# A two-layer graph attention kernel: one of seven products made with seven smaller ones, a bias put into the accumulators, ELU plus one, masks in halves and another schedule

## The chip, the cores and the metric

The kernel runs on one core of one Trainium2 chip. A core has TensorE (matmuls; PE in the profile, with its weight loads as PEld), VectorE (DVE), ScalarE (ACT), GpSimd (POOL) and SyncE (SP). Matmuls write to PSUM, eight banks of 512 f32 columns on 128 partitions; everything else lies in SBUF. The metric is device time in microseconds of one whole execution, for 32 graphs.

## The reference

```python
h = relu(layernorm(x))                 # x: (32, 512, 512) f32, adj: (32, 512, 512) int32
mask = (adj > 0) | eye(512)
def gat_layer(x, mask, W, a_src, a_dst, bias, concat):
    xl = (x @ W).reshape(B, N, H, F)
    e = leaky_relu(asrc[:, :, None, :] + adst[:, None, :, :], 0.2)   # asrc = <xl, a_src>, adst = <xl, a_dst>
    attn = softmax(where(mask, e, -1e9), axis=1)
    out = einsum('bsdh,bshf->bdhf', attn, xl)
    return out + bias                   # heads side by side if concat, else their mean
h = elu(gat_layer(h, mask, W1, ..., b1, concat=True))    # 4 heads of 256: 512 -> 1024
out = x + gat_layer(h, mask, W2, ..., b2, concat=False)  # 1 head: 1024 -> 512
```

All arithmetic on the large matrices is f32.

## The kernel before, in words

One graph is a batch of 512 nodes, held as four tiles of 128 rows. Per batch there are four large matrix products: the first projection (512 x 512 by 512 x 1024), the gather of layer 1 (per head, attention 512 x 512 by features 512 x 256), the second projection (512 x 1024 by 1024 x 512) and the gather of layer 2 (512 x 512 by 512 x 512). Two scalars per head, the scores of the attention, come out of the projections as extra columns, so the first has 258 columns per head and the second 257 per half.

**Seven products.** Each of these is cut into 2 x 2 blocks and made with seven block products instead of eight (Strassen's scheme in Winograd's form). `sums` makes the four sums of the left blocks (s1 = a21 + a22, s2 = s1 - a11, s4 = a12 - s2, and a21 becomes a11 - a21); `sums_of_weights` makes those of the weights once. `sevens` (line 814 on) runs over pairs of a unit (which part of the block's rows and columns) and a product number: a product is `kh` matmuls of 128 x 128 weights by 256 to 258 columns, two deep in the first projection and in the gathers, four deep in the second projection. Products share three accumulators per unit: 1, 6, 7, 4 go into bank `a`, 5 and 3 into `b`, 2 into `g`. After every product its partial sum is evicted to SBUF: products 1, 4, 5 and 6 by a ScalarE copy into their block (with sign -1 in the projections), 2, 3 and 7 by a VectorE addition or subtraction onto theirs. Batch 0 alone has its first projection and gather in plain form (`project1_first`, `gather1_plain`).

**The order.** The program first writes down all jobs with their reads, writes and an estimated cost (`prog.add`, by the helpers `act` at line 379, `dve` at 382, `dma` at 385, `accumulate` at 390 and `pe` at 396, which is why nearly all instructions of the profile carry one of these lines). TensorE keeps the written order. For the other engines and the two DMA queues (SyncE's, and GpSimd's for accumulating DMAs) `Program.order` simulates the chip with the costs, tries orders forwards and backwards, and keeps the one in which TensorE's products come soonest. The result is a fixed instruction stream per engine. It models DMAs as one wire with a lead and a tail:

```python
DMA_LEAD, DMA_TAIL, AHEAD = 0.8, 2.0, 3.5
```

PSUM banks come from a queue of eight: the one that was given back longest ago is taken first.

**Stages around the change.** In the main loop, round i does the second layer of batch i, the first gather of batch i+1 in pairs of heads (`PAIRS_OF`), the first projection of batch i+2 and the normalisation of batch i+3. Of the projection's 28 products, 14 run before the second pair of heads is gathered and 14 after it, in the order `FOUR`: two units, then two more.

- `masks` (line 504) turns four adjacency tiles into 0 or -2^100 in bf16 (`m`), sets the diagonal, writes the whole mask to DRAM (`dm`), and transposes it in two DMAs into `mt`. The transposed one enters the column minimum in `Soft.first`; the one in DRAM is added to the scores by GpSimd's accumulating DMAs in `Soft.second`. For the last batch VectorE adds `m` itself.
- `Soft.spread` writes small score vectors to DRAM (`das`, `drr`) and reads them back as rows on all partitions (`as`, `rr`), through SyncE's queue.
- `elu` (line 923): `h1` holds a gathered head with its sign changed; ScalarE makes exp(b1 - h1), then relu(1 - that), and VectorE min(h1 - b1, that), which is -elu. The following projection changes the sign back.
- `residual` (line 1104) loads the rows of x and VectorE adds b2 to them (`t<-t,b_sb`), 0.6 us each; `gather2` adds the gathered sums to them and stores them.

Of the kernel before, what the change touches and what calls it, by code (L numbers as in the profile page):

```python
# [10 lines left out]
F32 = mybir.dt.float32  # L11
# [8 lines left out]
P = 128  # L20
# [23 lines left out]

class Program:
# [9 lines left out]
    DMA_LEAD, DMA_TAIL, AHEAD = 0.8, 2.0, 3.5  # L55
# [28 lines left out]
    def forwards(self, rank):  # L84
# [5 lines left out]
        ready_at, start, landed = [0.0] * n, [0.0] * n, 0.0  # L90
        free, soon, ready = defaultdict(float), defaultdict(list), defaultdict(list)
        tensor = deque(j for j in range(n) if jobs[j][0] == "PE")
        for j in range(n):
            if not left[j] and jobs[j][0] != "PE":
                heappush(soon[jobs[j][0]], (0.0, j))
        done = []
        while len(done) < n:
            j, t = self.next_job(rank, free, soon, ready, tensor, left, ready_at, landed - self.AHEAD)
            start[j] = t
            free[jobs[j][0]] = t + jobs[j][1]  # L100
            done.append(j)
            if jobs[j][4] is not None:
                landed = max(landed, t + jobs[j][1] + self.DMA_LEAD) + jobs[j][4]
            for s in after[j]:
                if jobs[j][4] is not None:
                    r = landed + self.DMA_TAIL
                else:
                    r = t + jobs[j][1] + self.latency(j, s)
# [3 lines left out]
                if not left[s] and jobs[s][0] != "PE":  # L112
                    heappush(soon[jobs[s][0]], (ready_at[s], s))
        return start, done, cause
# [18 lines left out]
    def backwards(self, rank):  # L133
# [9 lines left out]
        while True:  # L143
            for j in found:
                if jobs[j][4] is not None:
                    moving = max(moving, ready_at[j]) + jobs[j][4]
                    ready_at[j] = moving + self.DMA_LEAD
# [4 lines left out]
            j, t = self.next_job(rank, free, soon, ready, tensor, left, ready_at)  # L152
# [4 lines left out]
            for d in jobs[j][2]:  # L157
                later = self.DMA_TAIL if jobs[d][4] is not None else self.latency(d, j)
# [5 lines left out]
    def next_job(self, rank, free, soon, ready, tensor, left, ready_at, hold=0.0):  # L164

        best = None
        for e in ("PE", "ACT", "DVE", "POOL", "SP"):
# [10 lines left out]
            if e in ("SP", "POOL"):  # L178
                t = max(t, hold)
            if best is None or t < best[0]:  # L180
                best = (t, e)
        t, e = best
        if e == "PE":
            return tensor.popleft(), t
# [3 lines left out]
        return heappop(ready[e])[1], t  # L188
# [3 lines left out]
    def order(self):  # L192
# [8 lines left out]
        for j in reversed(range(n)):  # L201
            later = self.DMA_LEAD + self.DMA_TAIL + (jobs[j][4] or 0.0)
# [54 lines left out]
def tile_gat(  # L257
# [75 lines left out]
    b1_sb = sbuf.tile([P, 2, FT], F32, name="b1_sb")  # L333
    b2_sb = sbuf.tile([P, DO], F32, name="b2_sb")
# [5 lines left out]
    hs = sbuf.tile([P, 3, KH, N // 2], F32, name="hs")  # L340
# [3 lines left out]
    xrs = slots("xr", 4, [P, N])  # L344
# [1008 lines left out]
```

## Time and profile before

| | |
|---|---|
| median of 3 runs | 2785.93 us (2783.84 to 2788.35) |
| profiled execution, first to last instruction (span) | 2778.8 us |
| median less span | 7.1 us |
| TensorE busy, records | 2746.2 us, 12520 |
| VectorE busy, instructions | 2645.4 us, 6726 |
| ScalarE busy, instructions | 2304.3 us, 4870 |
| GpSimd busy | 324.7 us |
| granted TensorE clock, mean | 0.998 |
| DMA moved | 501.55 MB |

The page gives one execution's span and no other time of it; what lies around the span (7.1 us to the median) is start and end of the program. An f32 matmul shows as two records. A record lasts about 380 ns, but the next starts some 217 ns later, so the busy time of an engine is the union of its records, and the distance between starts is what an instruction really costs. VectorE and ScalarE instructions overlap in the same way, by about 0.1 us. A group's row gives the names of what is written and read (numbers left out), the shape, busy time, the mean of one, and the idle time just before, with what ended it; `w_sb` stands for either weight, `h` for `h1`.

### The profile page before, as it was taken

The page shows a single profiled execution, that of the slowest core. Times are in us where ns is not written, and L with a number is a line of the kernel's source. Part 1 is how long each engine was busy: PE and PEld are TensorE (multiplying, and loading weights), DVE is VectorE, ACT ScalarE, POOL GpSimd, SP SyncE. Part 2 cuts the span into 40 slices and gives each one's busy share as a digit, 9 for nine tenths or more (in the row PEclk, how much of TensorE's full clock was granted, in tenths as well). Part 3 has the DMA queues.
Part 4 walks back from the last instruction along what each step waited for, and adds up shares of the span by engine and source line. Part 5 has one row for each costly group of instructions (what it writes and reads, how often), then busy time and mean ns, then how long its engine had stood idle before and what let it go on. Part 6 is the DMA issues. An engine that isn't in the chain of part 4 may idle for free. (4 is left out here: it accounts for less than half of the span.)

```text
span 2778.8 us, 41571 instructions
## 1 busy us (share of the span) xinstructions
PE 2746.2 (99%) x12520; PEld 2373.9 (85%) x12520; DVE 2645.4 (95%) x6726; ACT 2304.3 (83%) x4870; POOL 324.7 (12%) x356
## 2 busy tenths in 40 slices
PE   7999999999999999999999999999999999999999
PEld 6688888888888888888888888888888888888887
DVE  7999999999999999999999999999999999998997
ACT  5988888889888888888888888888888888887883
POOL 0110111001111101111011101011110111101110
PEclk9999999999999999999999999999999999999999
DMA  7766767667777667676677766777666867678663
GB/s 228 171 176 178 201 174 199 171 175 181 191 194 174 179 165 203 177 186 184 172 192 184 196 168 175 178 189 195 183 175 175 202 166 202 157 189 182 169 158 107
DMA packets 370964, 501.55 MB, mean 180 GB/s; under 512 B 222260, under 2 KB 226868, under 8 KB 370740
## 3 DMA queue, kind: packets, MB, share of 16 engines
q1 hardware_dynamic: 324948, 332.16, 43.6%
q0 software_dynamic: 45792, 166.74, 25.2%
q8 instruction: 100, 1.64, 0.2%
q14 instruction: 124, 1.02, 0.1%
HBM read 315.89 MB, written 51.31 MB: 132 GB/s over the span
## 5 line engine op out<-in xcount | busy, mean ns | idle before, releaser
L396 PE MATMUL mm<-w_sb,hs 128*128 128x257 f32 (+2 forms) x3032 | 688.5, 381 | 4.9 <-DVE hs L382 2.5
L396 PEld LDWEIGHTS mm<-w_sb,hs 128*128 128x128 f32 x3032 | 575.8, 190 | 92.0 <-ACT xl L379 4.6
L390 POOL DMA_DIRECT2D p<-dm x314 | 276.2, 887 | 2346.3 <-DVE p L382 1600.3
L379 ACT ACTIVATE l<-as,z 128x512 f32<-128x512 f32 x640 | 442.8, 721 | 101.9 <-DMA as<-das 96.2
L379 ACT ACTIVATE l<-l,low 128x512 f32<-128x512 f32 x640 | 459.2, 721 | 49.1 <-DVE low L382 46.0
L396 PE MATMUL mm<-w_sb,ht 128*128 128x258 f32 x2112 | 481.4, 382 | 1.9 <-DVE xl L382 1.4
L396 PE MATMUL mm<-p,xl 128*128 128x256 f32 (+1 forms) x1984 | 468.0, 384 | 1.0 <-DVE h L382 0.8
L396 PE MATMUL mm<-w_sb,h 128*128 128x257 f32 x2056 | 467.8, 379 | 0.0
L379 ACT ACTIVATE p<-p,z 128x512 f32<-128x512 f32 (+1 forms) x636 | 427.2, 716 | 42.6 <-DMA p<-dm 28.1
L382 DVE SCALAR_TENSOR_TENSOR p<-rr,z 128x512 f32<-128x512 f32 (+1 forms) x636 | 449.0, 743 | 11.8 <-DMA rr<-drr 11.6
L396 PEld LDWEIGHTS mm<-w_sb,ht 128*128 128x128 f32 x2112 | 400.9, 190 | 61.8 <-DVE xl L382 4.1
L382 DVE CUSTOM_DVE_ANT_1 l<-l,mt 128x512 f32<-128x512 f32 x640 | 429.1, 685 | 12.0 <-ACT l L379 9.5
L396 PEld LDWEIGHTS mm<-w_sb,h 128*128 128x128 f32 x2056 | 389.4, 189 | 57.8 <-issue 0.5
L396 PEld LDWEIGHTS mm<-p,xl 128*128 128x128 f32 x1984 | 377.1, 190 | 61.7 <-issue 5.7
L379 ACT ACTIVATE xl<-mm 128x258 f32<-128x258 f32 (+2 forms) x748 | 279.8, 382 | 70.6 <-PE mm L396 68.7
L379 ACT ACTIVATE h<-mm 128x256 f32<-128x256 f32 x496 | 181.7, 378 | 91.0 <-PE mm L396 88.4
L382 DVE TENSOR_TENSOR xl<-xl,mm 128x258 f32<-128x258 f32 x558 | 222.8, 420 | 29.1 <-PE mm L396 24.3
L379 ACT ACTIVATE xr<-h,b_sb 128x512 f32<-128x512 f32 x248 | 176.7, 721 | 75.7 <-DVE h L382 72.0
L396 PE MATMUL mm<-t,hs 128*128 128x256 f32 x992 | 226.0, 380 | 2.9 <-ACT h L379 2.9
L396 PEld LDWEIGHTS mm<-t,hs 128*128 128x128 f32 x992 | 188.4, 190 | 29.9 <-ACT h L379 4.7
L382 DVE SCALAR_TENSOR_TENSOR h<-h,b_sb,xr 128x512 f32<-128x512 f32 x248 | 182.9, 747 | 3.2 <-ACT xr L379 3.1
L382 DVE TENSOR_TENSOR t<-mm,t 128x256 f32<-128x256 f32 (+1 forms) x424 | 172.8, 419 | 11.7 <-PE mm L396 10.5
(114 smaller groups left out, 3421.8 us busy)
## 6 DMA issues: line engine op xcount, KB each, us to landing
p<-dm POOLq DMA_DIRECT2D x314, 512.0 KB, 5.2
rr<-drr SPq DMA_DIRECT2D x159, 512.0 KB
x<-in_x_dram SPq DMA_DIRECT2D x129, 256.0 KB
adj<-in_adj_dram SPq DMA_DIRECT2D x128, 256.0 KB
as<-das SPq DMA_DIRECT2D x64, 512.0 KB
t<-in_x_dram SPq DMA_DIRECT2D x124, 256.0 KB
out_dram<-t SPq DMA_DIRECT2D x124, 256.0 KB
dm<-m SPq DMA_DIRECT2D x32, 512.0 KB
```

What stands on the lines that cost most here:

```text
L379: prog.add("ACT", cost, reads, writes, lambda: nc.scalar.activation(*a, **k))
L382: prog.add("DVE", cost, reads, writes, lambda: f(*a, **k))
L390: lambda: nc.gpsimd.dma_start(to, at, accum_op=OP.add), size,
L396: f(*a, **k)
```

## The change

- **First projection.** Product 2 (a12 by b21, 256 x 256 by 256 x 516) is not made as four units of two matmuls any more, but itself with seven smaller products (`low`), one matmul of 128 x 128 by 258 columns each. `low_weights` makes the sums of b21's blocks once, `low_sums` those of a12's blocks per batch on VectorE, 128 columns each. Three parts (two units and `low`) now run interleaved in the order `TOP`; 19 of 31 products come before the second pair of heads. For the second pair of units the results of product 2 wait in `later`, and product 1 of those units is added to them by VectorE. Where a further bank is free, the sum of the small product 1 is copied to it by ScalarE (`forked`).
- **Second bias in banks.** b2 is no longer added to x on VectorE. ScalarE copies it (`seeds`) into the banks of products 1 and 5 of the second projection, and these products add to it. Since the features are gathered with weights that sum to one, a bias on the features is a bias on the result. `bias2` corrects it once by the column sums of W2, with 16 matmuls.
- **ELU plus one.** The eviction of layer 1 applies the sign and b1 + 1; `elu` is then one Exp on ScalarE and one VectorE step, max(h1, min(exp(h1 - 1), 1)) = elu + 1. The Relu pass is gone. The added one is what the column sums of W2 correct.
- **Masks in halves.** `m` holds two tiles instead of four; each half is written to DRAM and transposed by itself, and an accumulating DMA waits only for its half. The last batch reads its mask back from DRAM (`m_last`).
- **s4 after s2.** In the second projection and the gathers s4 overwrites s2, after product 6 has read it.
- **Schedule.** The planner models two DMA wires that share bandwidth, with other leads, tails, transfer costs and a hold on how far ahead DMAs are issued. `Banks` takes a bank by the width that was last written. There are three `xr` buffers instead of four, and `gather2` takes its products in the order `NEAR`.

```diff
+class Banks:
...
+    def __init__(self, tiles):
+        self.tiles, self.free, self.wide = tiles, deque(range(len(tiles))), [0] * len(tiles)
+    def take(self, width=512, kept=0):
+        i = next((i for i in self.free if self.wide[i] >= kept), None)
+        if i is None:
+            return None
+        self.free.remove(i)
+        self.wide[i] = max(width, self.wide[i] if kept else 0)
+        return ("mm", i), self.tiles[i]
+    def give(self, key):
+        self.free.append(key[1])
...
     PAIRS = {("PE", "ACT"): 0.21, ("PE", "DVE"): 0.21, ("DVE", "POOL"): 0.58, ("POOL", "DVE"): 0.4}
-    DMA_LEAD, DMA_TAIL, AHEAD = 0.8, 2.0, 3.5
+    DMA_LEAD, DMA_TAIL, AHEAD = {"SP": 0.6, "POOL": 0.75}, {"SP": 1.2, "POOL": 1.2}, 3.5
+    ALONE = {"SP": 1.0, "POOL": 1.0}
+    SHARED = {0: {"SP": 0.44, "POOL": 0.62}, 1: {"SP": 0.3, "POOL": 0.62}}
+    TURN = 0.95
...
+    def low_weights():
+        r00, r10, r11 = (w1_sb[:, 1, k, j, :] for k, j in ((0, 0), (1, 0), (1, 1)))
+        t1, t2, t4 = (w1_low[:, i] for i in range(3))
+        sub = nc.vector.tensor_sub
+        dve(ADD, R_KEYS, ["low1"], sub, t1, R01, r00)
+        dve(ADD, [*R_KEYS, "low1"], ["low2"], sub, t2, r11, t1)
+        dve(ADD, R_KEYS, R_KEYS, sub, R01, r11, R01)
+        dve(ADD, [*R_KEYS, "low2"], ["low4"], sub, t4, r10, t2)
...
+    def low_sums():
+        (a11, a12), (a21, a22) = (
+            [(ht[:, KQ + k, m * P : (m + 1) * P], [("ht", m, 1)]) for k in range(KQ)] for m in range(2)
+        )
+        s1, s2, s4 = ((hl[:, i], [("hl", i)]) for i in range(3))
+        def op(f, to, u, v):
+            dve(0.2, u[1] + v[1], to[1], f, to[0], u[0], v[0])
+        op(nc.vector.tensor_add, s1, a21, a22)
+        op(nc.vector.tensor_sub, s2, s1, a11)
+        op(nc.vector.tensor_sub, a21, a11, a21)
+        op(nc.vector.tensor_sub, s4, a12, s2)
+        return {1: a11, 2: a12, 3: s4, 4: a22, 5: s1, 6: s2, 7: a21}
...
+    def bias2():
+        ok, ones = ts_.take()
+        ones = ones[:, :P]
+        dve(0.2, (), [ok], nc.vector.memset, ones, 1.0)
+        for c in range(2):
+            bk, bt = banks.take(W2H)
+            pe(
+                [ok, *(k for r in range(2) for k in (("w2", AT[r, c]), ("w2s", AT[r, c])))],
+                [bk], 2 * KH * W2H / 593,
+                [
+                    (mm, (bt[:, :W2H], ones, w2_sb[:, AT[r, c], k, :]),
+                     dict(start=(r == 0 and k == 0), stop=(r == 1 and k == KH - 1)))
+                    for r in range(2) for k in range(KH)
+                ],
+            )
...
     def masks(b):
...
+        every = [("m", t) for t in range(2)]
+        for g in range(2):
+            for t in range(2):
+                ak, a = adjs.take()
+                row = (2 * g + t) * P
+                dma(0.8, (), [ak], a, adj[b, row : row + P, :])
+                dve(
+                    0.34, [ak], [("m", t)], nc.vector.tensor_scalar,
+                    m[:, t, :], a, 0.0, -BIG, op0=OP.is_le, op1=OP.mult,
+                )
+                adjs.give(ak)
...
+                0.2, every, every, nc.vector.tensor_max,
+                blocks, blocks, diag[:, None, :].to_broadcast([P, 2, P]),
+            )
+            dma(
+                1.0, every, [mk + (g,)],
+                md[:, 2 * g : 2 * g + 2].rearrange("p t n -> p (t n)"), m.rearrange("p t n -> p (t n)"),
+            )
...
+        left = {1: a11, 2: a12, 3: s4, 4: a22, 5: s1, 6: s2, 7: a21}
+        def last():
+            op(nc.vector.tensor_sub, s4, a12, s2)
+        if s4 is s2:
+            left[0] = last
+        else:
+            last()
...
-    def sevens(left, right, rkeys, put, kh, units, width, order):
...
+    def sevens(left, right, rkeys, put, kh, units, width, order, seeds={}):
...
+        bank, sixth = {}, len({u for u, _ in order})
         for u, n in order:
             m = units[u][0]
-            acc, first = {1: "a", 2: "g", 5: "b", 6: "a", 7: "a", 3: "b", 4: "a"}[n], n in (1, 2, 5)
+            acc, first = ACC[n], n in (1, 2, 5)
             if first:
-                bank[u, acc] = banks.take()
+                bank[u, acc] = banks.take(width, M if n in seeds else 0)
             bk, bt = bank[u, acc]
             ps = bt[:, :width]
+            if first and n in seeds:
+                first = False
+                act(0.29, [seeds[n][1]], [bk], ps, seeds[n][0], AF.Copy)
...
+            sixth -= n == 6
+            if n == 6 and not sixth and 0 in left:
+                left[0]()
...
+    HALF = 19
+    TOP = (
+        (0, 1), (1, 1), ("low", 1), (0, 5), (1, 5), ("low", 5), (0, 6), (1, 6), ("low", 2), ("low", 6),
+        (0, 3), (1, 3), ("low", 3), (0, 7), (1, 7), ("low", 7), (0, 4), (1, 4), ("low", 4),
+        *((u + 2, n) for n in (1, 5, 6, 3, 7, 4) for u in range(2)),
+    )
...
     def project1(b, left):
...
+        def low_to(m, j):
+            return to(m, 0, 0, 0) if j == 0 else (later[:, m], [("later", m)])
+        bank = {}
+        for u, n in TOP:
+            low = u == "low"
+            acc, first = ACC[n], n in (1, 2, 5)
+            if low and n == 2 and forked:
+                first = False
+            elif first:
+                bank[u, acc] = banks.take(W)
+            bk, bt = bank[u, acc]
+            ps = bt[:, :W]
+            if low:
+                (a, akeys), (w, wkeys) = LOW[0][n], LOW[1][n]
+                pe(akeys + wkeys, [bk], W / 593, [(mm, (ps, a, w), dict(start=first, stop=True, skip_group_check=True))])
+                if n == 1:
+                    forked = banks.take(W, W)
+                    if forked:
+                        bank[u, "g"] = gk, gt = forked
+                        act(COPY, [bk], [gk], gt[:, :W], ps, AF.Copy)
+                    else:
+                        d, keys = low_to(0, 0)
+                        dve(ADD, [bk] + keys, keys, nc.vector.tensor_sub, d, d, ps)
+                else:
+                    d, keys = low_to(*BLOCK[n - 1])
+                    if n in (5, 6):
+                        act(COPY, [bk], keys, d, ps, AF.Copy, scale=-1.0)
+                    else:
+                        dve(ADD, [bk] + keys, keys, nc.vector.tensor_sub, d, d, ps)
+            else:
+                m, j = u % 2, u // 2
+                a, akeys = left[n]
+                pe(
+                    akeys + w1_keys(n - 1), [bk], KQ * W / 593,
+                    [
+                        (mm, (ps, a[:, k, m * P : (m + 1) * P], w1_sb[:, n - 1, k, j, :]),
+                         dict(start=(first and k == 0), stop=(k == KQ - 1), skip_group_check=True))
+                        for k in range(KQ)
+                    ],
+                )
+                d, keys = to(m, j, *BLOCK[n - 1])
+                if n == 1 and j == 1:
+                    dve(ADD, [bk, ("later", m)], keys, nc.vector.tensor_sub, d, later[:, m], ps)
+                elif n in (1, 4, 5, 6):
+                    act(COPY, [bk], keys, d, ps, AF.Copy, scale=-1.0)
+                else:
+                    dve(ADD, [bk] + keys, keys, nc.vector.tensor_sub, d, d, ps)
+            if n in (2, 3, 4):
+                banks.give(bk)
+            yield
...
-    def elu(g, places, at):
+    def elu(g):
         keys = [("h1", g, r) for r in range(2)]
         ek, e = xrs.take()
-        act(0.62, [*places, "b1"], [ek], e, at, AF.Exp, bias=b1_sb[:, 0, g : g + 1], scale=-1.0)
-        act(0.54, [ek], [ek], e, e, AF.Relu, bias=1.0, scale=-1.0)
+        act(0.62, keys, [ek], e, h1[:, g, :], AF.Exp, bias=-1.0)
         dve(
-            0.65, [*places, ek, "b1"], keys, nc.vector.scalar_tensor_tensor,
-            h1[:, g, :], at, b1_sb[:, 1, g : g + 1], e, op0=OP.add, op1=OP.min,
+            0.65, [*keys, ek], keys, nc.vector.scalar_tensor_tensor,
+            h1[:, g, :], e, 1.0, h1[:, g, :], op0=OP.min, op1=OP.max,
         )
...
-                elu(h * FPH + f, [bk], ps)
+                g = h * FPH + f
+                act(
+                    0.52, [bk, "b1"], [("h1", g, r) for r in range(2)], h1[:, g, :], ps, AF.Identity,
+                    bias=b1_sb[:, g : g + 1], scale=-1.0,
+                )
                 banks.give(bk)
+                elu(g)
...
             g = h * FPH + r
             to, key = h1[:, g, c * M : (c + 1) * M], ("h1", g, c)
             if n in (1, 4, 5, 6):
-                act(COPY, [bk], [key], to, ps, AF.Copy)
+                act(
+                    COPY, [bk, "b1"], [key], to, ps, AF.Identity, bias=b1_sb[:, g : g + 1], scale=-1.0,
+                )
             else:
-                dve(ADD, [bk, key], [key], nc.vector.tensor_add, to, to, ps)
+                dve(ADD, [bk, key], [key], nc.vector.tensor_sub, to, to, ps)
             if n in (2, 3, 4):
                 banks.give(bk)
             if n in (5, 6):
...
-                elu(g, [("h1", g, q) for q in range(2)], h1[:, g, :])
...
+            {1: (b2_sb[:, 0], "b2"), 5: (b2_sb[:, 1], "b2")},
         )
...
-            dma(0.75, [x2_key(b, 0, 0)], halves, xr, x[b, d * P : (d + 1) * P, :])
-            dve(0.59, [xk, "b2"], halves, nc.vector.tensor_add, xr, xr, b2_sb)
+            dma(0.8, [x2_key(b, 0, 0)], halves, xr, x[b, d * P : (d + 1) * P, :])
...
             left1 = sums(ht_blocks(), KQ, 0.59)
+            LOW[0] = low_sums()
             masks(i + 2)
             ahead = project1(i + 2, left1)
-            for _ in range(14):
+            for _ in range(HALF):
...
+            mk, md = MASK[B - 1]
+            prog.alias("m_last", [k for ix in range(7) for k in w1_keys(ix)])
+            dma(0.5, [mk + (q,) for q in range(2)], ["m_last"], m_last, md)
```

## The prediction

> **What bounds the kernel now.** First the page's head: how long each engine is busy.
>
> ```profile
> span 2778.8 us, 41571 instructions
> PE 2746.2 (99%) x12520; PEld 2373.9 (85%) x12520; DVE 2645.4 (95%) x6726; ACT 2304.3 (83%) x4870; POOL 324.7 (12%) x356
> ```
>
> TensorE is busy in 99% of the span, VectorE in 95%. Busy TensorE time overlaps itself, so I count records. Busy time by stretches (us, then PE, PEld, DVE, ACT, POOL busy with their counts, granted clock, DMA share, GB/s), a steady stretch and the last one:
>
> ```profile
> 400.00:700.00 300.00, 300.00 (x1385) 262.71 (x1384) 288.99 (x731) 254.89 (x545) 33.64 (x36) 1.00 0.66 177
> 2650.00:2779.00 129.00, 120.86 (x514) 97.76 (x512) 107.01 (x254) 74.03 (x164) 10.35 (x12) 0.98 0.46 131
> ```
>
> In the steady stretch 1385 records fill 300.00 us, 216.6 ns each, with no idle time. An f32 matmul leaves two records (12520 = 2 x 6244 matmuls + 32 transposes), so a matmul of 256 to 258 columns costs 0.433 us, and nothing but fewer matmuls shortens this stretch. The rest of the span is idle: 2778.8 - 2746.2 = 32.6 us. The waits of TensorE alone (who waited for whom: us in total, times, longest):
>
> ```profile
> PE mm L396 <- ACT x L379: 11.8, 2, 11.5
> PE mm L396 <- DVE hs L382: 3.9, 4, 2.2
> PE mm L396 <- ACT h L379: 3.1, 5, 1.6
> PE mm L396 <- ACT xl L379: 2.4, 4, 1.0
> PE mm L396 <- ACT w_sb L379: 2.2, 1, 2.2
> PE mm L396 <- ACT p L379: 1.7, 2, 1.2
> PE mm L396 <- DVE h L382: 1.5, 2, 0.8
> PE mm L396 <- DVE xl L382: 1.4, 3, 0.9
> ```
>
> 11.5 us stand before the first matmul and some 4.4 after the last; 32.6 - 15.9 = 16.7 us are waits in between, 9.7 ended by ScalarE (3.1 + 2.4 + 2.2 + 1.7 + 0.3 on a row not shown), 7.0 by VectorE. A wait also has an echo. The timeline of TensorE around the longest late one (start, us, then the group, in brackets the idle time before it):
>
> ```profile
> 2692.02 1.03 PE L396 MATMUL mm<-p,hs 128*128 128x256 f32 x4
> 2695.26 2.08 PE L396 MATMUL mm<-w_sb,xl 128*128 128x256 f32 x4 [2.21 <-ACT w_sb L379]
> 2697.13 1.80 PE L396 MATMUL mm<-p,xl 128*128 128x256 f32 x4
> 2698.76 1.03 PE L396 MATMUL mm<-t,hs 128*128 128x256 f32 x4
> ```
>
> After 2.21 us of idling four records take 2.08 and 1.80 us instead of 1.03: about 1.8 us more. The idle 2.18 us at 49.9 us do the same (24 records in 7.17 us, 5.38 elsewhere). So the recoverable sum is 16.7 + 2 x 1.8 = 20.3 us. The Trainium skill ("TensorE: Matmul & The Clock Gate", Part 1) puts the fall to half clock after an idle window of some 3.4 us; this trace falls after 2.2 us, and the measurement decides. By the page's rule alone neither wait would have an echo, and the recoverable sum would be 16.7 us.
>
> **The change, part by part.**
>
> *Matmuls.* In each of 31 batches (the first has its own projection) product 2 of the first projection is 4 units x 2 depths = 8 matmuls; it becomes 7 of depth 128 and the same width. 31 x 0.433 = 13.4 us less. The bias correction adds 2 x 8 matmuls once, before the plain gather of batch 0, where TensorE has no gap (stretch 75.8 to 103.8 us runs without idling): 16 x 0.433 = 6.9 us more. Counted in the built programs: 6244 matmuls become 6229. Net -6.5 us, all on the path.
>
> *VectorE.* Costs are distances between starts, since neighbours overlap: 0.60 us for 512 columns (start 2690.05 to 2690.65), 0.33 for 256 (2691.26 to 2691.59). Gone: 128 additions of the bias to the residual, 128 x 0.60 = 77 us. New: 62 + 62 accumulations by way of `later` less 32 others, 92 x 0.33 = 30; 124 sums of 128 columns, an estimate of 0.20 each from the same line (0.33 less half of 0.27), 25; the mask's diagonal in 64 halves instead of 32 whole, about 2; once-only work about 5. Net -15 us, half a microsecond per batch. The elu's last step keeps its form (747 ns in the row `h<-h,b_sb,xr`). VectorE so stays as far under TensorE as it was.
>
> *ScalarE.* The rows that price it (busy us, mean ns of one, idle before):
>
> ```profile
> L379 ACT ACTIVATE xr<-h,b_sb 128x512 f32<-128x512 f32 x248 | 176.7, 721 | 75.7 <-DVE h L382 72.0 <-DVE z L382 2.7
> L379 ACT ACTIVATE xr<-xr 128x512 f32<-128x512 f32 x256 | 157.9, 630 | 1.1
> L379 ACT ACTIVATE h<-mm 128x256 f32<-128x256 f32 x496 | 181.7, 378 | 91.0 <-PE mm L396 88.4 <-DVE p L382 0.5
> L379 ACT ACTIVATE xl<-mm 128x257 f32<-128x257 f32 x248 | 91.5, 375 | 61.4 <-PE mm L396 60.2
> ```
>
> A bias column costs 721 - 630 = 91 ns. Gone: 256 Relu passes at 0.54 (start to start, 2713.20 to 2713.74), 138 us, and the bias column of 256 Exp, 23. New: the bias column on 496 evictions `h<-mm`, 45 us; 128 seeds of 257 columns at 0.28, 36; 8 plain evictions, 5. Net -75 us. None of it is on the path by itself; it shortens what ends the 9.7 us of ScalarE waits, and the chain from a gathered head through elu to the next projection loses one 0.6 us step.
>
> *Seeds.* In the second projection products 1 and 5 of both units wait for a ScalarE copy into their bank, 4 per batch: bank free, 0.38 us of copy, matmul. Best end: nothing, the bank that comes free longest ago is taken. Worst end: all 128 on the path, 128 x 0.38 = 49 us. I take nothing: a product of this stage lasts 1.74 us (8 records), so a bank that was freed one product ago covers the copy. The Trainium skill ("PSUM — Partial Sum Buffer", The four PSUM rules) speaks against seeding by ScalarE: whether a matmul adds to what that engine wrote depends on a hidden bit, and a seed other than 0 should go through TensorE. No row of this profile shows it. By that rule the 128 seeds would be identity matmuls on the path, 128 x 0.433 = 55 us, and the sum near 2832.
>
> *Weights' and sums' extra steps.* At 47 us TensorE waits 2.18 us for `hs`. VectorE now has four 258-column steps on weights (1.3 us) and four 128-column sums (0.8) ahead in that neighbourhood; TensorE has one more 0.43 us product before it needs `hs`. Between 0 (other waits of that neighbourhood hide them) and 2.1, I take 2.1 - 0.4 = 1.7 us more, once.
>
> *Step s4 put off.* It now overwrites s2 after product 6 and must be done before product 3: 4 or 5 products of 0.87 us for one step of 0.33 to 0.60, 6.9 us for one of 1.2. Nothing, while VectorE's queue is less than 3 us late; a miss would stop TensorE once per gather.
>
> *Masks in halves, DMAs, schedule.* SyncE issues 34 more transfers (32 mask writes among them); a half mask now waits until the other half's write and transpose have read the two tiles. Behind them in SyncE's queue stand the spreads, which ScalarE awaits:
>
> ```profile
> ACT l L379 <- DMA as<-das: 96.2, 36, 6.3
> ```
>
> Such waits up to 6.3 us did not stop TensorE in the steady stretches, so I take 0; a spread later by more than that would. POOL's queue (12% busy) has the same number of accumulates, each now waiting for its half. The planner's new DMA figures and costs reorder all queues; that can take all 20.3 us of waits and echoes or add to them. I take half of ScalarE's 9.7, -4.9, for the 75 us that it is relieved of, and leave VectorE's.
>
> Sum: -6.5 + 1.7 - 4.9 = -9.7 us. The profiled span is 2778.8, so about 2769 there; the median of the runs is 7.1 above that span (start and end outside it, which the change leaves alone): 2785.9 - 9.7 = **2776 us**.
>
> **Rivals.**
> 1. *The new order only moves the waits.* 16.7 us are 0.6% of the span and come from where a plan misses the chip by a microsecond; another plan misses elsewhere. Waits and echoes then grow by about what is saved in matmuls, 6.5: 2786. For it: ScalarE's relief lies mostly where TensorE has no idle time anyway.
> 2. *Slower: banks run out in the first projection.* Its order keeps three units open instead of two, two banks each, 6 of 8 instead of 4, with 31 instead of 28 evictions per batch; the gathers on both sides must hand back their banks sooner, and TensorE waits at that seam in every batch. The trace has such waits at seams, 0.27 us (at 2562.5), 1.25 (at 1117.2) and 1.61 (at 2524.5). It decides from 9.7 / 31 = 0.31 us per batch; at 0.65 the time is 2785.9 - 6.5 + 20 = 2800. Against it: in the steady stretch the evictions keep up without a gap, and the freed bank waits only for a 0.38 us copy.
> 3. *All waits go*: 2785.9 - 6.5 - 20.3 = 2759.
>
> **How the numbers follow.** About 0.2% (5.6 us) is what a measurement of this kernel can tell from no change: 2780.4 to 2791.5 counts as the same. Forecast 0.58 and rival 3 0.06 make faster 0.64; rival 1 0.14; rival 2, with missed seeds or s4 steps in it, 0.22. The range goes from 2759, all waits gone, to 2797, where rival 2 costs 0.57 us a batch; below it 0.06, above it 0.12. The likeliest case alone has 2767 to 2780.
>
> **What would show it.** After: 12490 records of TensorE, 216.6 ns apart in steady stretches; `t<-t,b_sb` gone, `xr<-h` near 630 ns, `h<-mm,b_sb` near 470, ScalarE's busy time below 2240 us; VectorE's within 20 us of now. Waits of TensorE between 10 and 18 us without head and tail. I am wrong if TensorE idles in every batch at the same seam (rival 2), if `mm<-b_sb` ends its waits (seeds), if spreads stop it, or if the pitch of the matmuls changes.

## The result, and the profile after

The changed kernel takes 2784.94 us, the median of 12 runs (2778.04 to 2790.15), and the kernel before took 2784.89 in 12 runs beside it (2775.58 to 2793.31). The ratio is 0.9999, with a 95% interval of 0.9987 to 1.0012: no change that can be measured, where 9.7 us less were forecast. The profiled execution took 2789.86 us, about 5 above its median, and its span is 2788.1. In all 12 runs the time is 1.8 us above the span, so start and end take 1.8 us, not 7.1: the profiled execution of before took about 2780.6, 4.3 below its median. The two profiles thus stand 9 us further apart than the medians do, and what differs between them shows where time went rather than how much.

The head of the page of after (span, then busy time of each engine with its share and instructions):

```profile
span 2788.1 us, 41716 instructions
PE 2747.0 (99%) x12490; PEld 2361.8 (85%) x12490; DVE 2626.0 (94%) x6857; ACT 2244.9 (81%) x4751; POOL 328.0 (12%) x356
```

The 30 records are gone, 12520 to 12490, and at 216.5 ns they are the 6.5 us of the forecast. But TensorE is busy 0.8 us longer than before, so the records that are left have lost 7.3 us, and it idles 41.1 us instead of 32.6. Who waited for whom (us in total, times, longest):

```profile
PE mm L463 <- DVE xl L449: 12.8, 18, 2.1
PE mm L463 <- ACT x L446: 10.9, 2, 10.6
PE mm L463 <- ACT w_sb L446: 3.8, 1, 3.8
PE mm L463 <- ACT h L446: 3.6, 3, 2.1
PE mm L463 <- DVE hs L449: 1.9, 2, 1.5
PE mm L463 <- ACT xl L446: 1.7, 2, 1.2
PE mm L463 <- DVE h L449: 0.7, 1, 0.7
PE mm L463 <- ACT p L446: 0.5, 1, 0.5
PE mm L463 <- DVE xr L449: 0.5, 1, 0.5
```

Without the 10.6 us before the first matmul these are 25.8 us, against 17.0 before by the same count (the prediction's 16.7 leaves out 0.3 under ScalarE's `x`). The waits ended by ScalarE are what they were (0.3 + 3.8 + 3.6 + 1.7 + 0.5 = 9.9, before 10.0). Those ended by VectorE went from 7.0 to 15.9, and one line did it: `xl`, 1.4 us in 3 waits before, 12.8 in 18 after. Which matmuls stand behind it, and the groups that the prediction priced (busy us, mean ns of one, idle before them):

```profile
L463 PE MATMUL mm<-w_sb,ht 128*128 128x258 f32 x1802 | 428.9, 385 | 13.8 <-DVE xl L449 12.6 <-DVE xr L449 0.5
L446 ACT ACTIVATE h<-mm,b_sb 128x256 f32<-128x256 f32 x496 | 226.6, 471 | 144.5 <-PE mm L463 142.4 <-DVE hs L449 0.4
L449 DVE SCALAR_TENSOR_TENSOR h<-xr,h 128x512 f32<-128x512 f32 x256 | 171.2, 680 | 2.9 <-ACT xr L446 2.9
L446 ACT ACTIVATE xr<-h 128x512 f32<-128x512 f32 x256 | 159.2, 627 | 40.8 <-DVE h L449 39.2 <-DVE low L449 0.7
L446 ACT ACTIVATE mm<-b_sb 128x257 f32<-128x257 f32 x128 | 47.8, 378 | 51.1 <-DVE t L449 51.0
```

They are the first projection's, and of those the ones that read `ht` directly: products 1, 7 and 4 and the low products 1, 2 and 7 (before: products 1, 2, 7 and 4). By their place in the order of TensorE's records, all the waits for `xl` in this row, 12.6 us, stand at the start of a product 4. The timeline of one such place (start, us, then the group, in brackets the idle time before it), TensorE first, then VectorE and ScalarE over the same 5 us:

```profile
1201.92 2.89 PE L463 MATMUL mm<-w_sb,ht 128*128 128x258 f32 x12
1206.39 1.14 PE L463 MATMUL mm<-w_sb,ht 128*128 128x258 f32 x4 [1.58 <-DVE xl L449]
...
1202.78 0.76 DVE L449 TENSOR_TENSOR xl<-xl,mm 128x258 f32<-128x258 f32 x2 [0.16 <-ACT xl L446]
1205.32 0.69 DVE L449 TENSOR_TENSOR hs<-p 128x512 f32<-128x512 f32 x1 [1.78 <-ACT p L446]
1205.93 0.41 DVE L449 TENSOR_TENSOR xl<-xl,mm 128x258 f32<-128x258 f32 x1
...
1203.95 1.33 ACT L446 ACTIVATE p<-p,z 128x512 f32<-128x512 f32 x2
```

This is the second pair of units. The 12 records are both products 7 and the first product 4. The second product 4 adds into the bank in which its product 7 stands, so VectorE's eviction of 7 must come first. That eviction stands in VectorE's queue behind a sum for the next gather (`hs<-p`), which waits 1.78 us for ScalarE's `p`; the eviction starts at 1205.93 and TensorE goes on 0.46 us later. In the order of before both products 2 lay between 7 and 4, three products or 2.6 us in all; now there is one product (0.87 us) in the second pair, and a product and a low product (1.30 us) in the first. In the trace of before 24 such records, the products 7, 2 and 4 of a pair, run without a gap:

```profile
1198.47 5.38 PE L396 MATMUL mm<-w_sb,ht 128*128 128x258 f32 x24
```

To add such losses up by place I use the starts of TensorE's records in the trace: what lies between two starts beyond the pitch of that width (about 216 to 217.5 ns for 256 to 258 columns, 430 for 512) is put down to the product of the later one. It holds waits and slowed records together. Before has 32.2 us of it, 3.9 ahead of the projection's `ht` matmuls; after has 49.0, 25.7 of it there. Steady stretches without waits are as they were; in the last stretch TensorE idles 4.8 of 130 us, before 8.1 of 129 (busy time by stretch, as in the prediction):

```profile
500.00:600.00 100.00, 100.00 (x463) 87.54 (x462) 98.07 (x252) 79.44 (x169) 11.98 (x13) 1.00 0.69 181
2650.00:2780.00 130.00, 125.25 (x543) 103.04 (x542) 106.47 (x262) 76.96 (x172) 10.38 (x12) 0.99 0.50 142
```

### The profile page after: what moved, and what is told of

Read it like the earlier page. It is cut to its first block, busy times and chain, and to the rows that moved or that the text cites. A ratio compares the mean times of both kernels' runs of the same rounds, so it can differ in the third digit from the quotient of the medians.

```text
span 2788.1 us, 41716 instructions
## 1 busy us (share of the span) xinstructions
PE 2747.0 (99%) x12490; PEld 2361.8 (85%) x12490; DVE 2626.0 (94%) x6857; ACT 2244.9 (81%) x4751; POOL 328.0 (12%) x356
## 3 DMA queue, kind: packets, MB, share of 16 engines
q0 software_dynamic: 45792, 166.74, 25.2%
## 5 line engine op out<-in xcount | busy, mean ns | idle before, releaser
L463 PE MATMUL mm<-w_sb,hs 128*128 128x257 f32 (+2 forms) x3032 | 697.5, 381 | 3.8 <-DVE hs L449 1.9
L446 ACT ACTIVATE l<-as,z 128x512 f32<-128x512 f32 x640 | 439.9, 716 | 111.6 <-DMA as<-das 110.4
L446 ACT ACTIVATE l<-l,low 128x512 f32<-128x512 f32 x640 | 457.5, 718 | 34.4 <-DVE low L449 32.2
L446 ACT ACTIVATE p<-p,z 128x512 f32<-128x512 f32 (+1 forms) x636 | 430.9, 715 | 56.3 <-DMA p<-dm 45.8
L449 DVE SCALAR_TENSOR_TENSOR p<-rr,z 128x512 f32<-128x512 f32 (+1 forms) x636 | 447.6, 738 | 16.2 <-DMA rr<-drr 15.9
L463 PE MATMUL mm<-w_sb,ht 128*128 128x258 f32 x1802 | 428.9, 385 | 13.8 <-DVE xl L449 12.6
L463 PEld LDWEIGHTS mm<-w_sb,ht 128*128 128x128 f32 x1802 | 336.9, 190 | 80.2 <-DVE xl L449 29.7
L446 ACT ACTIVATE h<-mm,b_sb 128x256 f32<-128x256 f32 (+1 forms) x504 | 232.0, 474 | 144.7 <-PE mm L463 142.7
L446 ACT ACTIVATE xl<-mm 128x258 f32<-128x258 f32 (+2 forms) x686 | 253.8, 379 | 50.6 <-PE mm L463 47.8
L449 DVE TENSOR_TENSOR xl<-xl,mm 128x258 f32<-128x258 f32 (+1 forms) x526 | 212.4, 414 | 38.0 <-PE mm L463 29.2
L446 ACT ACTIVATE xr<-h 128x512 f32<-128x512 f32 x256 | 159.2, 627 | 40.8 <-DVE h L449 39.2
L463 PE MATMUL mm<-xl,p 128*128 128x256 f32 (+1 forms) x752 | 179.3, 387 | 0.0
```

What stands on the lines that cost most here:

```text
L446: prog.add("ACT", cost, reads, writes, lambda: nc.scalar.activation(*a, **k))
L449: prog.add("DVE", cost, reads, writes, lambda: f(*a, **k))
L463: f(*a, **k)
```

## The experiments

Three causes were put against each other at first. A: product 4 waits for the eviction of 7 because too little stands between. B: the planner's new figures for transfers make a worse order. C: VectorE, busy 94% of the span, is late as a whole, and the place is chance. The table has every run: median, ratio to the kernel before on the same chip with its interval, and from the profiled execution the losses of TensorE as above, in all and ahead of the `ht` matmuls.

| kernel | us | ratio | losses | of these `ht` |
|---|---|---|---|---|
| before | 2784.89 | 1 | 32.2 | 3.9 |
| after | 2784.94 | 0.9999 [0.9987, 1.0012] | 49.0 | 25.7 |
| 7 ahead of 3 | 2807.29 | 1.0073 [1.0053, 1.0093] | 66.8 | 36.0 |
| no low products | 2786.40 | 1.0006 [0.9994, 1.0019] | 37.2 | 2.4 |
| after, planner of before | 2794.51 | 1.0039 [1.0025, 1.0054] | 52.1 | 15.9 |
| before, 4 close behind 7 | 2809.39 | 1.0086 [1.0058, 1.0115] | 47.1 | 29.2 |
| 4 put off | 2811.48 | 1.0099 [1.0067, 1.0132] | 74.0 | 26.9 |
| bias with 2 matmuls | 2815.40 | 1.0113 [1.0100, 1.0126] | 79.0 | 38.8 |
| both of these | 2829.72 | 1.0164 [1.0151, 1.0178] | 96.9 | 47.3 |
| no seeds | 2815.66 | 1.0117 [1.0101, 1.0133] | 85.0 | 39.9 |
| reserve for transfers | 2787.53 | 1.0018 [0.9998, 1.0038] | 44.9 | 17.5 |
| reserve, 4 put off | 2807.28 | 1.0081 [1.0060, 1.0101] | 64.0 | 25.2 |
| same order, own bank for 4 | 2775.17 | 0.9961 [0.9947, 0.9976] | 38.7 | 5.6 |
| same order, no seeds | 2786.26 | 1.0001 [0.9987, 1.0015] | 44.2 | 24.8 |

**Product 7 ahead of product 3**, which puts both products 3 between 7 and 4.

```diff
-        (0, 3), (1, 3), ("low", 3), (0, 7), (1, 7), ("low", 7), (0, 4), (1, 4), ("low", 4),
-        *((u + 2, n) for n in (1, 5, 6, 3, 7, 4) for u in range(2)),
+        (0, 7), (1, 7), ("low", 7), (0, 3), (1, 3), ("low", 3), (0, 4), (1, 4), ("low", 4),
+        *((u + 2, n) for n in (1, 5, 6, 7, 3, 4) for u in range(2)),
```

> The changed kernel with one edit: in the first projection product 7 comes before product 3, so that another product stands between 7 and 4, which share a bank. Theory A (product 4 waits until VectorE has evicted product 7 from the same bank; with product 2 gone from between them only 0.87 to 1.3 us are left for it): the waits of TensorE on VectorE's xl fall from 12.8 us to below 4, the excess before products on ht falls by about 15 us, time 2765 to 2775 against 2785. Rival B (the planner's new DMA figures are at fault): the waits move elsewhere, time 2780 to 2790. Rival C (VectorE is the bound): VectorE's work is the same, so time within 3 us of 2785.

It is 22 us slower than before and after, which none of the three had. Its waits of TensorE:

```profile
PE mm L463 <- ACT xl L446: 17.7, 23, 2.6
...
PE mm L463 <- DVE xl L449: 6.5, 4, 3.9
```

The waits for VectorE's `xl` halve, and those for ScalarE's grow from 1.7 to 17.7 us: now 7 follows close on 6, which is in the same bank, and whose eviction is ScalarE's. In this order what the link from 7 to 4 gained, the link from 6 to 7 lost.

**Without the low products**: product 2 of the first projection is one product again, in the order of before. All else of the change stays.

```diff
-    HALF = 19
-    TOP = (... ("low", 1), ... ("low", 5), ... ("low", 4), ...)
+    HALF = 14
+    FOUR = LAST + tuple((u + 2, n) for u, n in LAST)
```

> The changed kernel without the smaller seven products: product 2 is made as before, in the order of before, with 14 products before the second pair of heads; all else as changed. 31 more matmuls, 13.4 us. Theory A: the waits under xl vanish with the tight order, so the time is 2785 + 13.4 - 20 = 2775 to 2782. Rival B: the waits stay, time 2792 to 2800. Rival C: VectorE has 56 us less work, time falls by as much as half of it.

It has 12552 records, 13.4 us of matmuls more than after, and takes the same time. The waits for VectorE's `xl` are gone, as A has it, but there are others (`hs`, 9.1 us), and A's 2782 isn't reached.

**After, ordered by the planner of before.**

```diff
-    DMA_LEAD, DMA_TAIL, AHEAD = {"SP": 0.6, "POOL": 0.75}, {"SP": 1.2, "POOL": 1.2}, 3.5
+    DMA_LEAD, DMA_TAIL, AHEAD = 0.8, 2.0, 3.5
...
```

> The changed kernel ordered by the planner of before (one DMA wire, its lead, tail and hold), the jobs and their costs as changed. Theory A: the products' order is written by hand and stays, so the waits under xl stay above 8 us and the time is 2780 to 2792. Rival B: the waits go, time 2765 to 2775.

9.6 us slower than after, and the waits under VectorE's `xl` are still 8.3 us in 12. So B isn't needed for these waits; the time is 2.5 us above A's range.

**Before, with 4 close behind 7**: the same matmuls, product 2 moved ahead of 3.

```diff
-        (0, 1), (1, 1), (0, 5), (1, 5), (0, 6), (1, 6), (0, 3), (1, 3), (0, 7), (1, 7), (0, 2), (1, 2),
+        (0, 1), (1, 1), (0, 5), (1, 5), (0, 6), (1, 6), (0, 2), (1, 2), (0, 3), (1, 3), (0, 7), (1, 7),
         (0, 4), (1, 4),
```

> The kernel before with one edit: in the first projection product 2 is moved ahead of product 3, so that only one product stands between 7 and 4, as in the changed kernel; no matmul more or less. Theory A: waits of TensorE on VectorE's xl grow from 1.4 us to 8 to 15, time 2793 to 2805 against 2785. Rivals B and C: the same work and the same planner, time within 4 us of 2785.

24.7 us slower, with 29.2 us of losses ahead of `ht` instead of 3.9. Its profiled execution was the fastest of its six, 2795.63, so the rest of the time isn't in the trace. A expects a loss at just this place, and of its 8.3 us of waits for `xl` in 17 nearly all stand at a product 4; the time is 4 us above A's range, though, and the planner orders all other queues anew around the moved products, and the next runs show what that alone can do.

**Product 4 put off** behind two products of the next gather, in both pairs, so that 1.7 us more lie between.

```diff
-            for _ in range(HALF):
+            for _ in range(HALF - 3):
                 next(ahead)
+            between = gather1(s, PAIRS_OF[1])
+            for _ in range(2):
+                next(between)
+            for _ in range(3):
+                next(ahead)
...
+            for _ in range(10):
+                next(ahead)
+            if i < B - 3:
+                residual(i)
+                behind = gather2(i, S2[i], sums2(i, S2[i]))
+                for _ in range(2):
+                    next(behind)
+            run(ahead)
```

> The changed kernel with more products between 7 and 4 in the first projection: the first pair's two products 4 and low product 4 come after the first two products of the next gather, the second pair's two products 4 after the first two products of the second layer's gather, where there is one. Matmuls, evictions and banks of each product stay. Theory A (product 4 waits for VectorE's eviction of product 7 from the same bank because too little stands between): the waits under VectorE's xl fall from 12.8 to under 5 us, the stalls ahead of the projection's matmuls from 25.7 to under 10, and the time to 2767 to 2777 us. Rival C (VectorE itself is the bound at 94%): the waits turn up at the next product that needs VectorE (the sums hs, or the gathers' products), and the time stays at 2781 to 2788. Rival E (ScalarE becomes the late one there, as when 7 was moved forward): waits under ScalarE's xl or h above 8 us, 2785 or more.

**The bias correction with 2 matmuls**, after VectorE has summed the weight blocks.

```diff
-                [bk], 2 * KH * W2H / 593,
-                [
-                    (mm, (bt[:, :W2H], ones, w2_sb[:, AT[r, c], k, :]),
...
+            for r in range(2):
+                for k in range(KH):
+                    ...
+                        dve(ADD, [jk, *w], [jk], nc.vector.tensor_add, ...)
+            pe(
+                [ok, jk], [bk], W2H / 593,
+                [(mm, (bt[:, :W2H], ones, junk[:, :W2H]), dict(start=True, stop=True))],
+            )
```

> The changed kernel with the bias correction's 16 matmuls cut to 2: VectorE first sums the eight weight blocks of each half (16 steps of 0.33 us, once), then one matmul of ones for each half. The prediction's step says that all 16 lie on TensorE's path: 14 x 0.433 = 6.1 us less, 2779. Rival: VectorE's 5.3 us more at that place are late themselves and TensorE waits there for what stands behind them in VectorE's queue: 2784 to 2786, with a new wait in the first 150 us.

**Both of these.**

> Both edits: the products 4 put off behind two products of the next gather, and the bias correction with 2 matmuls. If the two costs are separate and both theories hold, the gains add up: 2761 to 2771 us. If either falls, the time is that of the other alone.

**No seeds**: the ScalarE copies of the second layer's bias into the banks are left out.

```diff
             lambda n: [("w2", n - 1), ("w2s", n - 1)], signed(to, 1.0), KH, [(0,), (1,)], W2H, TWO,
-            {1: (b2_sb[:, 0], "b2"), 5: (b2_sb[:, 1], "b2")},
         )
```

> The changed kernel with the second projection's products 1 and 5 unseeded: the 128 copies of the bias into the banks by ScalarE are left out, and with them the second layer's bias in the output. The prediction's step costs the seeds at nothing: 2782 to 2788 us, waits as before. The other end, each seed on the path with 0.38 us: 2736. In between, a seed is late only sometimes: 2770 to 2782.

All four are 27 to 45 us slower than after; of what was expected only rival E of the first allows that. With product 4 put off, waits for VectorE's `xl` are 16.3 us in 6 instead of 12.8 in 18, those for ScalarE's `xl` 8.5, as rival E had it; but their longest are 5.8 and 5.6 us, which no distance of 1.7 us covers. All 16.3 us still stand at a product 4, of the second pair: the product that waits is the same, and the eviction of 7 comes later than the added distance. With 2 bias matmuls the first 200 us lose 29.6 instead of 13.0 us, and `ht` loses 38.8 all over the span, where the bias has no part. The last is the telling one, since it only leaves 128 copies out. Its page and its waits:

```profile
span 2823.8 us, 41540 instructions
PE 2759.3 (98%) x12490; PEld 2368.7 (84%) x12490; DVE 2629.0 (93%) x6857; ACT 2206.6 (78%) x4623; POOL 324.3 (11%) x356
```

```profile
PE mm L463 <- DVE xl L449: 20.6, 21, 3.4
PE mm L463 <- DVE hs L449: 17.4, 9, 4.7
```

ScalarE does 38 us less, VectorE does the same, and TensorE waits for VectorE in new places. The planner computes the order of ScalarE's, VectorE's and the DMA queues from all costs at once, so one job less makes another order of thousands; without seeds the banks are chosen differently, too. None of these runs shows the price of its own edit alone, and the four before them share that doubt. Hence two kinds of run for the last four: two more orders, and two in which every queue keeps exactly the order of after (in their traces TensorE, VectorE, ScalarE and GpSimd run the same sequence of instructions as in after, the seeds aside).

**Reserve for transfers.** In after, late links often begin with ScalarE waiting for a transfer (`l <- DMA as<-das` 110.4 us in 55 waits, before 96.2 in 36; `p <- DMA p<-dm` 45.8, before 28.1). If the new figures plan transfers too close, counting more for each should help.

```diff
-    DMA_LEAD, DMA_TAIL, AHEAD = {"SP": 0.6, "POOL": 0.75}, {"SP": 1.2, "POOL": 1.2}, 3.5
+    DMA_LEAD, DMA_TAIL, AHEAD = {"SP": 0.6, "POOL": 0.75}, {"SP": 2.0, "POOL": 2.0}, 3.5
```

> The changed kernel ordered with more reserve for transfers: the planner counts 2.0 us instead of 1.2 from the end of a transfer until what reads it may start, for both queues (the planner of before counted 2.0). The work is the same; only the order of the queues differs. Theory F (the new figures leave no reserve, a transfer that lands a microsecond late stops ScalarE, then VectorE's queue, then product 4): the waits of TensorE under VectorE's xl fall from 12.8 to under 6 us, 2768 to 2779. Rival G (any new order of these queues is as good or bad as chance makes it, as the five reordered kernels from 2795 to 2830 suggest): 2785 to 2830, with the waits in other places. Theory A alone (product 4 too close behind 7 whatever the order) says that stalls ahead of the projection's matmuls stay above 20 us.

**Reserve, and product 4 put off.**

> Both: 2.0 us of reserve for transfers in the planner, and the products 4 of the first projection put behind two products of the next gather, as in the run that widened the distance alone. If reserve and distance are both wanted (theories A and F): 2763 to 2775, stalls ahead of the projection's matmuls under 8 us. If chance of the order decides (rival G): 2785 to 2830.

Reserve by itself brings nothing: `xl` still ends 11.3 us in 13 waits, and 2787.53 is what G allows and F doesn't. The losses ahead of `ht` fall to 17.5, though, where A alone said above 20. With product 4 put off as well it is slower again, as G has it.

**Same order, own bank for product 4.** The jobs are emitted in the list of after's order; product 4 starts anew in the bank of 5 and 3, which is kept until then, while the bank of 1, 6 and 7 goes back after 7; so later products get other banks as well.

```diff
-        for j in self.order():
+        for j in pinned():
...
             acc, first = ACC[n], n in (1, 2, 5)
+            if n == 4:
+                acc, first = "b", True
...
-            elif first:
+            elif first and n != 4:
                 bank[u, acc] = banks.take(W)
...
-            if n in (2, 3, 4):
+            if n in (2, 7, 4):
                 banks.give(bk)
```

> The changed kernel with every queue in exactly its order, kept as a list, and one thing taken away: product 4 of the first projection (and the low product 4) starts anew in the bank that products 5 and 3 used, so that it does not wait for the eviction of product 7. What 1, 6 and 7 had summed is missing from its output. Theory A: the stalls ahead of the projection's matmuls fall from 25.7 to under 8 us and the time to 2763 to 2775. Rival C (VectorE is late as a whole): what product 4 no longer waits for turns up at the next wait for VectorE, 2780 to 2788.

This is the run that tells A from C. Its page, its waits, and the timeline of the place shown above (TensorE, then VectorE):

```profile
span 2778.3 us, 41742 instructions
PE 2743.7 (99%) x12490; PEld 2366.0 (85%) x12490; DVE 2621.8 (94%) x6857; ACT 2240.3 (81%) x4751; POOL 326.9 (12%) x356
```

```profile
PE mm L463 <- DVE xl L449: 2.3, 6, 0.9
PE mm L463 <- DVE hs L449: 2.3, 2, 2.0
PE mm L463 <- DVE later L449: 2.0, 2, 1.4
```

```profile
1197.24 3.76 PE L463 MATMUL mm<-w_sb,ht 128*128 128x258 f32 x16
1200.84 1.89 PE L463 MATMUL mm<-xl,p 128*128 128x256 f32 x8
...
1200.64 0.69 DVE L449 TENSOR_TENSOR hs<-p 128x512 f32<-128x512 f32 x1 [1.78 <-ACT p L446]
1201.25 0.42 DVE L449 TENSOR_TENSOR xl<-xl,mm 128x258 f32<-128x258 f32 x1
```

VectorE stands the same 1.78 us for ScalarE's `p`, and evicts product 7 just as late. But TensorE runs its 16 records of 7 and 4 in 3.76 us and goes on into the gather: the wait was the shared bank's. Waits for `xl` fall from 12.8 to 2.3 us. The time falls by 9.8 us against after and by 10.9 against the runs of before beside it, at the same distance of the profiled execution from the median (+4.9 in both). The losses say where the rest stayed: 20.1 us less ahead of `ht`, but 4.5 more ahead of `hs`, 2.8 ahead of low products, 1.9 ahead of the bias matmuls and some in smaller places, 10.3 less in all. The 2.8 come from the edit itself: low product 4 now stands behind low product 3 in a bank and twice waits for its eviction (`later`). The largest single wait ahead of `hs`, 1.91 us at 1368.21, is for ScalarE. So A holds: the wait is the shared bank's, and taking it away is worth 9.8 us, though 2775.17 lies just above A's range. About half of the 20.1 us turns up elsewhere, a part of it behind VectorE, as C says; how much of it is VectorE's lateness, one execution of each doesn't show.

**Same order, no seeds.**

```diff
-                act(0.29, [seeds[n][1]], [bk], ps, seeds[n][0], AF.Copy)
+                prog.add("ACT", 0.29, [seeds[n][1]], [bk], lambda: None)
+                first = True
```

> The changed kernel with every queue in exactly its order, kept as a list, and the 128 copies of the second layer's bias into the banks left out (the output lacks that bias). It is the work of the earlier run without seeds, in the order of the changed kernel. Seeds cost nothing, as predicted, and the earlier run's 31 us came from its new order: 2781 to 2788. Seeds late now and then: 2770 to 2780. If leaving them out is itself slower by some other way, as the earlier run would say taken alone: about 2815.

```profile
span 2783.5 us, 41582 instructions
PE 2747.4 (99%) x12490; PEld 2362.2 (85%) x12490; DVE 2625.6 (94%) x6857; ACT 2206.9 (79%) x4623; POOL 327.3 (12%) x356
```

The same 4623 ScalarE instructions as the earlier run without seeds, and 2786.26 us instead of 2815.66. The seeds cost nothing that can be measured, and 29 us of the earlier run were its order and its choice of banks.

What stays open is why the reordered kernels spread from 2786 to 2830 us and none falls below after. One thing that the planner has wrong is seen in the trace: it counts 0.28 us for the eviction `h<-mm,b_sb`, as before, and back to back they now start 0.36 us apart. Whether that spreads the orders wasn't tried. Nor was a wider distance between 7 and 4 in a kept order, so no run shows that distance alone would do. Before has the shared bank too, and 1.4 us of these waits in an execution 4.3 us under its median; what it would gain from a bank of its own is not shown. Nor was a version tried that keeps product 4's sum and gives it a bank of its own; the run shows what it could win, 9.8 us, before the addition that VectorE would then have to make.

## Why the prediction was right or wrong

The time lies in the range, and within 1.1 us of rival 1's 2786, but the likeliest case was wrong: 2776 forecast as faster, 2784.9 and no change measured. By its steps:

- *Matmuls, -6.5*: right. 12490 records at an unchanged pitch, and the bias correction is wholly on the path, 32 records without a gap where TensorE goes straight on:

```profile
73.25 7.12 PE L463 MATMUL mm<-w_sb,t 128*128 128x257 f32 x32
```

- *VectorE, -15*: right in size, 2645.4 to 2626.0, but partly by luck: an estimate from the distances between starts puts some 15 of these 19.4 us on the elu step (256 x 0.06), which the prediction kept, so its own terms came to little. That it "stays as far under TensorE as it was" was right in the sum and beside the point: what it does late matters by who waits.
- *ScalarE, -75*: its rows came as told (`xr<-h` 627 ns, `h<-mm,b_sb` 471), the sum was 59.4, to 2244.9 instead of under 2240; which term fell short isn't shown.
- *Seeds, 0*: right, by the run with the same order. The sum near 2832, from the rule on seeds that spoke against them, didn't come.
- *`hs` at 47 us, +1.7*: wrong in sign; the matmuls on `hs` start at 48.24 without a wait, so 2.2 us and their echo went. A new wait of 2.08 for `xl` at 72.28 is one of those at a product 4. *s4 put off, 0*: no wait of that kind shows. *Masks, DMAs, queues, 0*: right in the steady stretches as far as could be seen, but at 2684.97 TensorE waits 3.79 us for a ScalarE that had stood 3.40 us for a transfer (`p<-dm`).
- *"I take half of ScalarE's 9.7, -4.9"*: wrong. ScalarE's waits are 9.9. What it was relieved of shortened no wait of TensorE in sum. Rival 1 had said so, and the forecast took it too lightly.
- *The step that failed* is the one that isn't in the sum. The prediction counted the products of the first projection and their evictions, and not how far apart the products of one bank stand. Taking product 2 away took the filler between 7 and 4. The run with the same order puts it at 9.8 us: without this wait the kernel takes 2775.17. That this is within 1 us of the forecast 2776 is chance, since two of the three terms of the sum, +1.7 and -4.9, were wrong.
- *Rival 2* named the right stage and a wait that comes back; it had it in every batch, and the trace of after has 18 for 31. Its mechanism, banks that run out at the seam, isn't what happened: the bank was held, and its own next product waited for its eviction. *Rival 1* had the right time, and by the medians TensorE did lose about what the matmuls save, 6.5; but its reason, another plan that misses elsewhere, isn't what was shown: the wait comes from the order of products, which is written by hand, and stays under the planner of before. That loss and gain are equal is luck.
- *"7.1 above that span ... start and end outside it"*: wrong. About 1.8 us lie there; the rest, about 5 us, was the scatter of one execution against the median. The sum was added to the median of the runs, so the time doesn't suffer from it; but the waits of 20.3 us that it hoped to shorten were read from an execution 4 us under the median, and the effect that was to be predicted is of that size.

## What to carry to other kernels

When a product is taken out of a chain that accumulates in one bank, ask what it stood between: look in the order for the next pair that shares a bank, count the time between them, and set it against the longest that the evicting engine is seen to stand still in its queue (here 0.87 us against 1.78). The runs show that taking the shared bank away helps; that more distance would too, only before and the run without low products suggest, which have 2.6 us there and few of these waits. Where a planner orders the queues, an experiment that changes a job changes the whole order; keep the order as a list before an edit is priced, since otherwise leaving work out can cost 29 us. Take a few us of difference from medians, and use the single profiled execution for where, not for how much.

## What the runs showed of the hardware that was not expected

- TensorE's records after a wait, over the 14 traces. A gap here is the distance between two starts beyond the pitch, 0.16 us more than the idle time of a profile's row, and counts where the 32 records before it lost less than 0.25 us together. After 253 gaps of up to 2.1 us the next 32 records lose 0.11 us in the median and never more than 0.97. After 26 gaps over 2.7 us they always lose 1.55 to 3.15 us, in 7 to 14 slow records. Between the two lie 13 gaps; six of them cost 1.8 to 1.9, the others at most 0.97. The Trainium skill ("TensorE: Matmul & The Clock Gate", Part 1) puts the fall to half clock after an idle window of some 3.4 us and says that the number of slow matmuls at a kernel's start varies from run to run. Here the number varies from gap to gap. By the idle time of the profile slow records come after as little as 2.02 us, and 2.47 us went by without them: the fall lies sooner than the page has it, and the measurement decides. Waits of a microsecond, which most of the waits of after are, cost hardly more than themselves each.
- VectorE's elu step of 512 columns became shorter with the change, 747 to 680 ns and from 0.66 to 0.60 us start to start, although the prediction kept it. Its column of biases became the constant 1.0, and one of its two operations another; `p<-rr,z`, which still reads a column, starts 0.66 us apart in the same trace. No run changed the column alone.
